# Feed-forward: several outputs share the early chunks, the late chunks follow; the last projection is stepped from an earlier place

## The chip, the cores and the metric

One core of a Trainium2 chip runs the whole program. The metric is the device time of one execution in microseconds (us). Six names recur: PE (the matmul engine; its weight loads are PEld), DVE (VectorE), ACT (ScalarE), POOL (GpSimd) and SP, whose queue (SPq) issues the DMAs spoken of here.

## The reference

The input x is 4096 rows of 256. An attention layer (16 heads of 16, causal) with its norms comes first and gives a new x; the feed-forward that the change touches follows:

```
x = x + layernorm(attention(layernorm(x)))
n = layernorm(x)
h = silu((n @ w1.T) * s1) * ((n @ w2.T) * s2)     # 256 -> 1024
h = gelu((h @ h1.T) * sh1)                        # 1024 -> 1024
h = gelu((h @ h2.T) * sh2)                        # 1024 -> 1024
y = (h @ w3.T) * s3                               # 1024 -> 256
x = x + layernorm(y)
```

The matrices w1, w2, h1, h2 and w3 hold -1, 0 and 1 alone.

## The kernel before

**Blocks and parts.** The 4096 rows are NB = 8 blocks of QB = 512. In the feed-forward, activations lie transposed: features on the 128 partitions, the block's 512 rows along the free axis. So 1024 features are FC = 8 chunks, 256 features are DC = 2. Since the matrices hold small whole numbers, each activation is split into a high part rounded to a matmul-friendly format and a low part that is the rest (`settle`, L974 to L978: a cast and a subtraction on DVE). Each product is thus made twice, once with each part, and both go into the same PSUM bank. The tiles are called ha (the output of w1/w2) and hb_0, hb_1 (those of h1 and h2), with h or l for the part. The function is built twice, for parts = 2 and parts = 1; a flag chooses at run time, and the profiled execution takes parts = 2.

**A block.** The loop over j goes through five stages, in this order on PE:

- w1/w2: for each of 8 outputs (oc), 4 matmuls into a bank za and 4 into a bank zb (`linear`, matmul at L1007). ACT applies silu to za (sl, L1046), DVE multiplies sl with zb (fa, L1048) and settles the result.
- h1: for each of 8 outputs, 16 matmuls (8 chunks, 2 parts) into a bank z. ACT applies gelu (fb, L1063) and DVE settles.
- h2: the same once more.
- the last projection of the feed-forward: for each of 4 row tiles t, 16 matmuls of 256 columns into a bank pyf (L1076). DVE multiplies by s3 (yf, L1083) and takes the norm's statistics (L138, L139).
- `leave`: the norm's root on POOL (rstd, L173), the normalisation on DVE (L1025), the addition of x on POOL (L1029) and the store to HBM on SP (L1032). In the last block it is done tile by tile.

Banks za, zb, z and pyf come in turn from a pool of six PSUM banks (`ps_f`); a bank is free again when ACT or DVE has read it. `f2` holds two tiles each of sl, and of the full result before it is split.

**The order.** A manual schedule is on for all five engines: the instructions of an engine run in the order in which the program's text issues them, and one that waits holds up everything behind it on its engine.

**Background work.** `Background` (L27) keeps a queue of generators. Each `step` runs the first of them to its next `yield`, and goes on to the next generator in the same step when the first has ended. `finish` runs all that is left. In the feed-forward there is a step after each output of w1/w2, h1 and h2, and two after those of h1 and h2 in block 1. Two kinds of work are in it:

- `project(NB - 1, room)` (L213), once, in block 1: the attention's last projection for the last block. Its pieces: a load of x and a load of the softmax sums (L222); after three empty steps the reciprocal on DVE (L225); then, in one piece, the store of the reciprocals (invd, L227) and four loads into oi (L231, L232), which share their buffers with the transposed input xTf of a block; after three empty steps two products on POOL (L239), a step each; two empty steps; two pieces of 8 matmuls py (L249), each with an addition and statistics on DVE (L258, L138); then the root (ve on DVE, L171, and rstd on POOL) and for each of four row tiles a normalisation and an addition on POOL (L177, L286); last, the store of the new x (L288).
- `norm_block(j + 1, ...)` (L291), in every block but the last: the load of the next block's x (L113), two empty steps, four pieces of statistics, then root and normalisation (yn, L177 on DVE) and in a last piece 8 transposing matmuls (ptf, L308) and the split into xTf (ACT L992, DVE L994).

In block 1 norm_block stands in the queue behind project.

Of the kernel before, what the change touches and what calls it, by code (L numbers as in the profile page):

```python
# [3 lines left out]

# [6 lines left out]
F32 = mybir.dt.float32  # L11
# [6 lines left out]
P = 128  # L18
QB = 512
NT = QB // P  # L20
# [47 lines left out]
def sandwich_kernel(  # L68
# [19 lines left out]
    nc = tc.nc  # L88
    S, D = x.shape
# [6 lines left out]
    NB = S // QB  # L96
    DC = D // P
    FC = F // P
# [37 lines left out]
    def layernorm_stats(src, mv, t):  # L136
        st = stat.tile([P, nc.vector.BN_STATS_DIM], F32, tag="bn", name="bn")
        nc.vector.bn_stats(st, src)  # L138
        nc.vector.bn_aggr(mv[:, t, :], st)  # L139
# [71 lines left out]
    PREP, PROJECT, NORM = 26, 28, 12  # L211
# [79 lines left out]
    def norm_block(j, room, done):  # L291

        xj = xb[j] = load_block(0, x1[j])
        for _ in range(3):
            yield True
        mv = stat.tile([P, NT, 2], F32, tag="mv", name=f"mvf_{j}")
        for t in range(NT):
            layernorm_stats(xj[:, t, :], mv, t)
            yield True
        rstd = layernorm_rstd(mv)  # L300
        xh = room.tokens(j)
        for t in range(NT):
            normalize(xh[:, t, :], xj[:, t, :], mv, rstd, t)
        yield True
        pts = [room.bank(f"ptf_{j}_{c}") for c in range(DC)]
        for c in range(DC):
            for t in range(NT):
                nc.tensor.transpose(  # L308
                    pts[c][:, t * P : (t + 1) * P], xh[:, t, c * P : (c + 1) * P], ident
                )  # L310
        done(pts)
        yield True
# [25 lines left out]
    with ExitStack() as actx:  # L338
# [13 lines left out]
        def two_banks(name):  # L352
            return ps_s.tile([P, 2, QB], F32, tag="s", name=name)
# [430 lines left out]
        bg = Background(lambda: unit_beside())  # L784
        halving = halve_weights()
        actx.enter_context(tc.manual_schedule(engines=ALL_ENGINES))
        room = Room()
# [26 lines left out]
        ahead, begun_pair, item = [], [], (0, 0)  # L814

        def unit_beside():
            j, g = item
            if not begun_pair and 1 <= j < NB - 1 and g < G - 1 and len(ahead) < NT:
                begun_pair.extend(next(stream))
                ahead.append(1)  # L820
            if begun_pair:
                issue(MaxUnit(*begun_pair.pop(0)))
# [6 lines left out]
        ps = two_banks("pb")[:, 0, 0:D]  # L829
        for c in range(DC):  # L830
            nc.tensor.matmul(
                ps,
                lhsT=bv[:, c : c + 1].to_broadcast([P, P]),
                rhs=wp[:, c, :],
                start=(c == 0),
                stop=(c == DC - 1),
# [73 lines left out]
    def feed_forward(halves):  # L910
# [5 lines left out]
        parts = 2 if halves else 1  # L916
        with ExitStack() as fctx:
# [4 lines left out]
            ps_f = fctx.enter_context(tc.tile_pool(name="ps_f", bufs=6, space=PSUM))  # L922
# [3 lines left out]
            def single(ap):  # L926

                return ap.bitcast(F32R) if halves else ap
# [15 lines left out]
            w3_r = fw.tile([P, FC, D], F32R, tag="w3", name=f"w3_{parts}")  # L944
            w3_sb = w3_r.bitcast(F32)
            room, bg = Room(), Background()
# [7 lines left out]
            def weights(key, oc, kc):  # L954

                if halves:
                    at = slice(oc % 4 * P, (oc % 4 + 1) * P)
                    return [tiles[key][c, oc // 4][:, at] for c in range(kc)]
                w = f2.tile([P, FC, P], F32, tag="raw", name=f"{key}_{oc}")
                src = sources[key][:, oc * P : (oc + 1) * P]  # L960
                nc.sync.dma_start(out=w[:, 0:kc, :], in_=src.rearrange("(c p) f -> p c f", p=P))
                return [w[:, c, :] for c in range(kc)]

            def activations(n, name):

                return [
                    (f1 if halves and n == DC else hp).tile(
                        [P, n, QB], F32, tag=f"h{n}{p}", name=f"{name}{p}"
                    )
                    for p in "hl"[:parts]  # L970
                ]

            def settle(dst, c, full):

                if halves:
                    hi, lo = (single(d[:, c, :]) for d in dst)
                    nc.vector.tensor_copy(hi, full)  # L977
                    nc.vector.tensor_tensor(lo, full, hi, ALU.subtract)  # L978

            def chunk(dst, c, name):  # L980

                if not halves:
                    return dst[0][:, c, :]
                return f2.tile([P, QB], F32, tag="full", name=name)
# [14 lines left out]
                            )  # L999
                return done  # L1000

            def linear(key, oc, src, kc, name):
                ps = ps_f.tile([P, QB], F32, tag="f", name=name)
                w = weights(key, oc, kc)
                for c in range(kc):
                    for i, part in enumerate(src):
                        nc.tensor.matmul(  # L1007
                            ps,
                            lhsT=w[c],
                            rhs=single(part[:, c, :]),  # L1010
                            start=(c == 0 and i == 0),
                            stop=(c == kc - 1 and i == parts - 1),
                        )
                return ps

            xTs[0] = [t.bitcast(F32) for t in xT0]
            if not halves:
# [21 lines left out]
            for j in range(NB):  # L1039
                xT = xTs[j]  # L1040
                ha = activations(FC, f"ha{parts}_{j}")
                for oc in range(FC):
                    za = linear("w1", oc, xT, DC, f"za{parts}_{j}_{oc}")
                    zb = linear("w2", oc, xT, DC, f"zb{parts}_{j}_{oc}")
                    sl = f2.tile([P, QB], F32, tag="sl", name=f"sl{parts}_{j}_{oc}")
                    nc.scalar.activation(sl, za, AF.Silu, scale=s1[:, oc : oc + 1])  # L1046
                    h = chunk(ha, oc, f"fa{parts}_{j}_{oc}")
                    nc.vector.scalar_tensor_tensor(  # L1048
                        h, zb, s2[:, oc : oc + 1], sl, ALU.mult, ALU.mult
                    )  # L1050
                    settle(ha, oc, h)
                    bg.step()
                if j == 1:
                    bg.add("project", project(NB - 1, room), PROJECT)
                if j + 1 < NB:
                    bg.add("norm", norm_block(j + 1, room, keep_features(j + 1)), NORM)
                src = ha
                for layer, (key, sc) in enumerate((("h1", sh1), ("h2", sh2))):
                    hb = activations(FC, f"hb{parts}_{j}_{layer}")
                    for oc in range(FC):  # L1060
                        z = linear(key, oc, src, FC, f"z{parts}_{j}_{layer}_{oc}")
                        h = chunk(hb, oc, f"fb{parts}_{j}_{layer}_{oc}")
                        nc.scalar.activation(h, z, AF.Gelu, scale=sc[:, oc : oc + 1])  # L1063
                        settle(hb, oc, h)
                        bg.step()
                        if j == 1:
                            bg.step()
                    src = hb
                bg.finish()
                y = f1.tile([P, NT, D], F32, tag="yf", name=f"yf{parts}_{j}")  # L1070
                mv = stat.tile([P, NT, 2], F32, tag="mv", name=f"mvo{parts}_{j}")
                for t in range(NT):
                    ps = ps_f.tile([P, QB], F32, tag="f", name=f"pyf{parts}_{j}_{t}")
                    for c in range(FC):
                        for i, part in enumerate(src):
                            nc.tensor.matmul(  # L1076
                                ps[:, 0:D],
                                lhsT=single(part[:, c, t * P : (t + 1) * P]),
                                rhs=(w3_r if halves else w3_sb)[:, c, :],
                                start=(c == 0 and i == 0),  # L1080
                                stop=(c == FC - 1 and i == parts - 1),
                            )
                    nc.vector.tensor_tensor(y[:, t, :], ps[:, 0:D], s3, ALU.mult)  # L1083
                    layernorm_stats(y[:, t, :], mv, t)
                    if j == NB - 1:

                        one = slice(t, t + 1)
                        due.append((j, y, mv, one, layernorm_rstd(mv[:, one, :])))
                        while len(due) > (t < NT - 1):
                            leave(*due.pop(0))  # L1090
                if j < NB - 1:
                    leave(j, y, mv, slice(0, NT), layernorm_rstd(mv))
# [3 lines left out]
    with tc.If(low < 1) as either:  # L1096
        feed_forward(True)
# [36 lines left out]
```

## Time and profile before

| what | us |
|---|---|
| median of 3 runs | 2488.5 |
| lowest and highest run | 2483.43, 2493.22 |
| profiled execution | 2495.86 |
| its span, first to last instruction | 2494.2 |
| first za matmul of the feed-forward | 1798.00 from the span's start |
| first pyf matmul of the last block | 2477.60 |

The page of the profile gives each engine's busy time and its share of the span. PE's row must be read with care: matmuls overlap, a 128x512 one is shown busy for 0.39 us while the next one starts 0.2266 us after it, so a gap in the starts can be larger than the idle time shown. Timelines list instructions in order of time, with the idle time of the engine before one and what ended it in brackets. Shares of time in the feed-forward by block, from the first matmul of each stage to that of the next, as the timeline gives them:

| block | w1/w2 | h1 | h2, with ptf | pyf to the next block |
|---|---|---|---|---|
| 0 | 15.04 | 29.05 | 30.81 | 8.15 |
| 1 | 14.53 | 34.86 (py in it) | 36.45 | 8.15 |
| 2 | 14.54 | 32.98 | 30.78 | 8.15 |
| 3 | 14.53 | 31.45 | 30.78 | 8.15 |
| 4 | 14.54 | 31.43 | 30.78 | 8.15 |
| 5 | 14.54 | 32.96 | 30.78 | 8.14 |
| 6 | 14.54 | 31.43 | 30.78 | 8.14 |
| 7 | 14.54 | 31.44 | 29.01 (no ptf) | - |

### The profile page before, as it was taken

The numbers are of one execution on the slowest core, as the hardware profiler recorded it, in microseconds if no ns is written. First come the engines' busy times: TensorE is split into PE (matmuls) and PEld (weight loads), VectorE is DVE, ScalarE is ACT, GpSimd is POOL, SyncE is SP. The second block draws the span as 40 slices with busy tenths as digits, with TensorE's granted clock in tenths as the row PEclk, the third lists the DMA queues.
The fourth block names the chain that finished last, engine by engine and source line by source line (L and its number), as shares of the span: only waits on it lengthen the run. The fifth ranks groups of instructions, "written<-read, shape, count | busy, mean of one in ns | idle before, by whom it ended". The sixth has DMA issues, their size and how long they took to land.

```text
span 2494.2 us, 40139 instructions
## 1 busy us (share of the span) xinstructions
PE 2395.7 (96%) x15237; PEld 1434.2 (58%) x15237; DVE 1786.7 (72%) x3838; ACT 1309.1 (52%) x1710; POOL 561.6 (23%) x898
## 2 busy tenths in 40 slices
PE   4899999999999999999999999999999999999998
PEld 2545545545554555455555555544488787887887
DVE  1667988888897989799999888986145535554553
ACT  1336666665675667666667667766822222222221
POOL 2325333423343233322422222000001200000000
PEclk8779999999999999999999999999999999999999
DMA  4444434323333322424222231111111100000000
GB/s 145 150 141 141 151 115 152 120 82 130 107 126 117 116 72 96 151 94 133 84 74 72 88 109 60 51 56 56 47 54 35 34 1 18 17 17 1 17 9 10
DMA packets 134825, 202.73 MB, mean 81 GB/s; under 512 B 14912, under 2 KB 59584, under 8 KB 134624
## 3 DMA queue, kind: packets, MB, share of 16 engines
q1 hardware_dynamic: 132672, 198.75, 24.3%
q8 instruction: 122, 2.00, 0.3%
q10 hardware_dynamic: 1776, 1.18, 0.2%
q14 instruction: 79, 0.65, 0.1%
q0 software_dynamic: 176, 0.15, 0.1%
HBM read 137.91 MB, written 62.13 MB: 80 GB/s over the span
## 4 chain that ended last, share of the span: by engine, by line
PE 82%; DVE 11%; issue 2%; DMA 2%; ACT 1%; POOL 1%; SPq 0%; ACTq 0%; POOLq 0%; DVEq 0%
PE av L714 20%; PE s L664 18%; PE z L1007 18%; PE pm L581 16%; DVE mx L594 3%; DVE pm L598 2%; PE pyf L1076 2%; DVE fa L1048 2%; PE pk L426 1%; PE py L249 1%; PE pv L543 1%; PE pq L426 1%; PE pmt L630 1%; PE za L1007 1%; PE zb L1007 1%
## 5 line engine op out<-in xcount | busy, mean ns | idle before, releaser
L679 ACT ACTIVATE e<-s 128x1024 f32<-128x1024 f32 (+3 forms) x1175 | 1039.1, 936 | 471.1 <-PE s L664 462.3
L594 DVE TENSOR_REDUCE mx<-pm 128x1 f32<-128x512 f32 x1792 | 1111.5, 682 | 153.0 <-PE pm L581 135.4
L581 PE MATMUL pm<-k,q 64*128 64x512 f32 (+3 forms) x2304 | 626.9, 456 | 33.0 <-DVE mx L594 18.6
L581 PEld LDWEIGHTS pm<-k,q 64*128 64x128 f32 x2304 | 325.1, 188 | 533.3 <-DVE mx L594 368.9
L714 PE MATMUL av<-e,v 128*32 128x512 f32 (+3 forms) x4608 | 582.5, 577 | 0.2 <-POOL e L684 0.2
L664 PE MATMUL s<-q,k 64*128 64x512 f32 (+3 forms) x2304 | 472.7, 391 | 4.4 <-ACT xT L533 1.2
L664 PE MATMUL s<-mrow,ones 64*128 64x512 f32 (+3 forms) x2304 | 458.9, 381 | 0.0
L598 DVE CUSTOM_DVE_ANT_0 pm<-pm,mask 128x384 f32<-128x384 f32 (+3 forms) x512 | 240.2, 517 | 78.6 <-PE pm L581 75.7
L1063 ACT ACTIVATE fb<-z,sh 128x512 f32<-128x512 f32 x128 | 88.1, 688 | 388.4 <-PE z L1007 367.2
L664 PEld LDWEIGHTS s<-q,k 64*128 64x128 f32 x2304 | 236.5, 189 | 71.7 <-issue 18.8
L664 PEld LDWEIGHTS s<-mrow,ones 64*128 64x128 f32 x2304 | 241.3, 189 | 38.3 <-DVE mrow L638 0.7
L684 POOL TENSOR_SCALAR_AFFINE_SELECT e<-e 128x256 f32<-128x256 f32 x256 | 102.3, 407 | 620.1 <-ACT e L679 618.0
L1007 PE MATMUL z<-hb_0h,h 128*128 128x512 f32 x512 | 200.8, 392 | 0.0
L1007 PE MATMUL z<-hb_0l,h 128*128 128x512 f32 x512 | 200.0, 391 | 0.0
L714 PEld LDWEIGHTS av<-e,v 128*32 128x32 f32 x4608 | 91.7, 108 | 143.6 <-issue 130.5
L173 POOL TENSOR_TENSOR rstd<-ve,neghalf 128x4 f32<-128x4 f32 (+1 forms) x22 | 20.7, 943 | 662.9 <-DVE ve L171 637.4
L977 DVE CAST hb_1h<-fb 128x512 fp32r<-128x512 f32 x64 | 27.8, 435 | 144.5 <-ACT fb L1063 144.5
L977 DVE CAST hb_0h<-fb 128x512 fp32r<-128x512 f32 x64 | 27.3, 427 | 138.7 <-ACT fb L1063 138.7
L1007 PEld LDWEIGHTS z<-hb_0h,h 128*128 128x128 f32 x512 | 96.8, 189 | 20.0
L1046 ACT ACTIVATE sl<-za,s 128x512 f32<-128x512 f32 x64 | 44.0, 689 | 122.2 <-PE za L1007 64.2
L1007 PEld LDWEIGHTS z<-hb_0l,h 128*128 128x128 f32 x512 | 96.7, 189 | 19.9
L1048 DVE SCALAR_TENSOR_TENSOR fa<-zb,s,sl 128x512 f32<-128x512 f32 x64 | 47.6, 745 | 72.2 <-ACT sl L1046 72.2
(247 smaller groups left out, 2437.8 us busy)
## 6 DMA issues: line engine op xcount, KB each, us to landing
k<-k SPq DMA_DIRECT2D x288, 256.0 KB
q<-q SPq DMA_DIRECT2D x64, 256.0 KB
x<-in_x_dram SPq DMA_DIRECT2D x16, 512.0 KB
k<-hik SPq DMA_DIRECT2D x32, 256.0 KB
k<-lok SPq DMA_DIRECT2D x32, 256.0 KB
q<-hiq SPq DMA_DIRECT2D x32, 256.0 KB
q<-loq SPq DMA_DIRECT2D x32, 256.0 KB
avd<-av_sb SPq DMA_DIRECT2D x32, 256.0 KB
```

The source lines that it names most:

```text
L426: nc.tensor.matmul(ps, lhsT=wqk[d][:, i * D + c * P : i * D + (c + 1) * P], rhs=xTs[j][:, d, :], start=(d == 0), stop=(d == DC - 1),)
L581: nc.tensor.matmul(ps[:, 0:n], lhsT=qT[j, g][pr][r, t * P : (t + 1) * P], rhs=kT[G * j + g, c, pr][r, 0:n], start=True, stop=True,)
L594: nc.vector.tensor_reduce(self.mx[:, h, c : c + 1], ps[:, 0:n], AX.X, ALU.max)
L598: nc.vector.tensor_tensor_reduce(out=ps[:, 0:n], in0=ps[:, 0:n], in1=mask[:, QB - n : QB], scale=1.0, scalar=-3.0e38, op0=ALU.add, op1=ALU ...
L664: nc.tensor.matmul(self.ps[i][:, self.q0 :], lhsT=(self.k, ones[pr])[m][r, :], rhs=(qT[j, g][pr], mT[j, g])[m][r, self.q0 :], start=(m == ...
L679: nc.scalar.activation(e[:, at : at + n, q0:], ps[:, :, q0:], AF.Exp)
L684: nc.gpsimd.affine_select(out=at, in_=at, compare_op=ALU.is_ge, fill=0.0, base=0, pattern=[[0, 2], [1, P]], channel_multiplier=-1,)
L714: nc.tensor.matmul(self.av[h * HW : (h + 1) * HW, q0:], lhsT=vb[kt // NT][:, kt % NT, o : o + HW], rhs=es[h // 2][:, h % 2, q0:], start=(k ...
L977: nc.vector.tensor_copy(hi, full)
L1007: nc.tensor.matmul(ps, lhsT=w[c], rhs=single(part[:, c, :]), start=(c == 0 and i == 0), stop=(c == kc - 1 and i == parts - 1),)
L1048: nc.vector.scalar_tensor_tensor(h, zb, s2[:, oc : oc + 1], sl, ALU.mult, ALU.mult)
L1063: nc.scalar.activation(h, z, AF.Gelu, scale=sc[:, oc : oc + 1])
```

## The change

`linear` becomes a generator over a list of outputs. It takes the banks of all of them at once, runs the first kc - late chunks for each output in turn, and then the last `late` chunks for each, handing an output over as it is complete. In h1, with two parts, the first three outputs are made so with late = 3: chunks 0 to 4 of outputs 0, 1 and 2, then chunks 5 to 7 of each. All other outputs of w1/w2, h1 and h2 are made as before. The last projection does the same with its first two row tiles and late = 2. The sums and their order within a bank stay as they were.

`project` is put into the queue of block 1 ahead of the loop over w1/w2, not behind it, so that loop's eight steps work on it; and behind each output of h1 and h2 in block 1 there are three steps, not two.

```diff
-            def linear(key, oc, src, kc, name):
-                ps = ps_f.tile([P, QB], F32, tag="f", name=name)
-                w = weights(key, oc, kc)
-                for c in range(kc):
-                    for i, part in enumerate(src):
-                        nc.tensor.matmul(ps, lhsT=w[c], rhs=single(part[:, c, :]),
...
-                return ps
+            def linear(key, ocs, src, kc, name, late=0):
+                banks = [ps_f.tile([P, QB], F32, tag="f", name=f"{name}_{oc}") for oc in ocs]
+                ws = [weights(key, oc, kc) for oc in ocs]
+                for cs in filter(len, (range(kc - late), range(kc - late, kc))):
+                    for ps, w in zip(banks, ws):
+                        for c in cs:
+                            for i, part in enumerate(src):
+                                nc.tensor.matmul(ps, lhsT=w[c], rhs=single(part[:, c, :]),
...
+                        if cs.stop == kc:
+                            yield ps
...
                 ha = activations(FC, f"ha{parts}_{j}")
+                if j == 1:
+                    bg.add("project", project(NB - 1, room), PROJECT)
                 for oc in range(FC):
...
                     bg.step()
-                if j == 1:
-                    bg.add("project", project(NB - 1, room), PROJECT)
                 if j + 1 < NB:
                     bg.add("norm", norm_block(j + 1, room, keep_features(j + 1)), NORM)
...
-                    for oc in range(FC):
-                        z = linear(key, oc, src, FC, f"z{parts}_{j}_{layer}_{oc}")
+                    ahead = 3 if halves and layer == 0 else 1
+                    name = f"z{parts}_{j}_{layer}"
+                    for oc, z in enumerate(
+                        chain(
+                            linear(key, range(ahead), src, FC, name, 3 if ahead > 1 else 0),
+                            *(linear(key, [oc], src, FC, name) for oc in range(ahead, FC)),
+                        )
+                    ):
...
-                        bg.step()
-                        if j == 1:
+                        for _ in range(1 + 2 * (j == 1)):
                             bg.step()
...
-                for t in range(NT):
-                    ps = ps_f.tile([P, QB], F32, tag="f", name=f"pyf{parts}_{j}_{t}")
-                    for c in range(FC):
...
+                def outputs(ts, late=0):
+                    banks = {t: ps_f.tile([P, QB], F32, tag="f", name=f"pyf{parts}_{j}_{t}") for t in ts}
+                    for cs in filter(len, (range(FC - late), range(FC - late, FC))):
+                        for t, ps in banks.items():
+                            for c in cs:
...
+                            if cs.stop == FC:
+                                yield t, ps
+                for t, ps in chain(outputs(range(2), 2), *(outputs([t]) for t in range(2, NT))):
                     nc.vector.tensor_tensor(y[:, t, :], ps[:, 0:D], s3, ALU.mult)
```

More of the change, by code (lines that the diff above doesn't have):

```diff
@@ L2 @@
 from contextlib import ExitStack
-from itertools import cycle
+from itertools import chain, cycle
 import concourse.bass as bass
@@ L1000, in keep_features @@
                 return done
-            def linear(key, oc, src, kc, name):
-                ps = ps_f.tile([P, QB], F32, tag="f", name=name)
-                w = weights(key, oc, kc)
-                for c in range(kc):
-                    for i, part in enumerate(src):
[L1007 to L1013, printed above, removed]
-                return ps
+            def linear(key, ocs, src, kc, name, late=0):
[5 more added lines that the diff above has]
+                            for i, part in enumerate(src):
+                                nc.tensor.matmul(
+                                    ps,
+                                    lhsT=w[c],
+                                    rhs=single(part[:, c, :]),
+                                    start=(c == 0 and i == 0),
+                                    stop=(c == kc - 1 and i == parts - 1),
+                                )
+                        if cs.stop == kc:
+                            yield ps
             xTs[0] = [t.bitcast(F32) for t in xT0]
@@ L1041, in feed_forward @@
                 ha = activations(FC, f"ha{parts}_{j}")
+                if j == 1:
+                    bg.add("project", project(NB - 1, room), PROJECT)
                 for oc in range(FC):
-                    za = linear("w1", oc, xT, DC, f"za{parts}_{j}_{oc}")
-                    zb = linear("w2", oc, xT, DC, f"zb{parts}_{j}_{oc}")
+                    za, = linear("w1", [oc], xT, DC, f"za{parts}_{j}")
+                    zb, = linear("w2", [oc], xT, DC, f"zb{parts}_{j}")
                     sl = f2.tile([P, QB], F32, tag="sl", name=f"sl{parts}_{j}_{oc}")
@@ L1059, in feed_forward @@
                     hb = activations(FC, f"hb{parts}_{j}_{layer}")
-                    for oc in range(FC):
-                        z = linear(key, oc, src, FC, f"z{parts}_{j}_{layer}_{oc}")
+                    ahead = 3 if halves and layer == 0 else 1
[4 more added lines that the diff above has]
+                            *(linear(key, [oc], src, FC, name) for oc in range(ahead, FC)),
+                        )
+                    ):
                         h = chunk(hb, oc, f"fb{parts}_{j}_{layer}_{oc}")
@@ L1071, in feed_forward @@
                 mv = stat.tile([P, NT, 2], F32, tag="mv", name=f"mvo{parts}_{j}")
-                for t in range(NT):
-                    ps = ps_f.tile([P, QB], F32, tag="f", name=f"pyf{parts}_{j}_{t}")
-                    for c in range(FC):
[L1075 to L1082, printed above, removed]
+                def outputs(ts, late=0):
[3 more added lines that the diff above has]
+                            for c in cs:
+                                for i, part in enumerate(src):
+                                    nc.tensor.matmul(
+                                        ps[:, 0:D],
+                                        lhsT=single(part[:, c, t * P : (t + 1) * P]),
+                                        rhs=(w3_r if halves else w3_sb)[:, c, :],
+                                        start=(c == 0 and i == 0),
+                                        stop=(c == FC - 1 and i == parts - 1),
+                                    )
+                            if cs.stop == FC:
+                                yield t, ps
+                for t, ps in chain(outputs(range(2), 2), *(outputs([t]) for t in range(2, NT))):
                     nc.vector.tensor_tensor(y[:, t, :], ps[:, 0:D], s3, ALU.mult)
```

## The prediction

> **What bounds the kernel now.** First the page: which engine is full.
>
> ```profile
> PE 2395.7 (96%) x15237; PEld 1434.2 (58%) x15237; DVE 1786.7 (72%) x3838; ACT 1309.1 (52%) x1710; POOL 561.6 (23%) x898
> ```
>
> PE carries the chain that ended last (82% of it). The programs of both kernels are the same up to the feed-forward, so only 1798.00 (first za) to 2494.2 can change. There I asked who PE waited for; the columns are total us, times, longest.
>
> ```profile
> PE ptf L308 <- DVE yn L177: 3.7, 1, 3.7
> PE pyf L1076 <- DVE hb_1l L978: 1.8, 8, 0.2
> PE z L1007 <- DVE ha_7h L977: 0.9, 2, 0.6
> ```
>
> These idles look like pennies, but matmuls overlap: a 128x512 one is busy 0.39 and the next starts 0.2266 later. So I read start to start. PE's timeline where block 1 begins h1:
>
> ```profile
> 1898.08 0.39 PE L1007 MATMUL z<-ha_1l,h 128*128 128x512 f32 x1
> 1898.65 0.50 PE L1007 MATMUL z<-ha_1h,h 128*128 128x512 f32 x1 [0.18 <-DVE ha_1h L977]
> 1899.37 0.51 PE L1007 MATMUL z<-ha_1l,h 128*128 128x512 f32 x1 [0.22 <-DVE ha_1l L978]
> 1900.50 0.50 PE L1007 MATMUL z<-ha_1h,h 128*128 128x512 f32 x1 [0.62 <-DVE ha_1h L977]
> 1901.22 0.50 PE L1007 MATMUL z<-ha_1l,h 128*128 128x512 f32 x1 [0.22 <-DVE ha_1l L978]
> 1901.56 0.39 PE L1007 MATMUL z<-ha_1h,h 128*128 128x512 f32 x1
> ```
>
> Output 0 needs chunks 6 and 7 while DVE still makes them. Its 16 matmuls start at 1895.58, the next output's at 1901.56: 5.98 instead of 3.63, so 2.35 lost. Then the granted clock, from the table of windows (us; PE, PEld, DVE, ACT, POOL; PEclk; DMA):
>
> ```profile
> 1895.58:1901.56 5.98, 4.73 (x18) 2.92 (x16) 5.38 (x10) 1.98 (x2) 0.00 (x0) 1.00 0.00 0
> 1952.20:1961.10 8.90, 5.16 (x17) 3.99 (x16) 3.96 (x9) 1.86 (x3) 1.03 (x1) 0.62 0.00 0
> 1989.58:1998.60 9.02, 7.77 (x24) 5.32 (x23) 6.49 (x12) 2.66 (x3) 0.00 (x0) 0.82 0.01 2
> 2062.00:2076.00 14.00, 14.00 (x63) 11.60 (x62) 12.37 (x23) 4.82 (x7) 4.04 (x5) 1.00 0.23 75
> ```
>
> Block 2's stall (third row) is followed by a slow stretch, matmuls 0.43 apart for some 3.4 us; block 1's (first row) is not.
>
> **Late chunks in h1 (removes a stall).** From first z<-ha to first z<-hb, the timeline gives block 0 29.05 us (128 x 0.2266: no stall) and blocks 2 to 7 32.98, 31.45, 31.43, 32.96, 31.43, 31.44. Above 29.03 that is 3.95, 2.42, 2.40, 3.93, 2.40, 2.41: 17.5 together, of which some 3.0 are the slow stretches in blocks 2 and 5. The same 128 matmuls run after; three outputs first take chunks 0 to 4 (30 x 0.2266 = 6.80 us), then the rest. Chunk 5 is wanted 6.80 after the start, chunk 7 7.7 after; in block 1 chunk 7's low half came 5.6 after (1901.2 - 1895.58), in block 3 5.7. About 2 us of cover: stall zero. Next in line is a bank: output 1 starts 2.27 after and takes zb 5's, freed 0.7 after (fa 5 ends 1896.28). DVE meets three outputs 1.36 apart with 1.1 us of work each and keeps up. **-17.5**; block 1 -2.35.
>
> **Late chunks in the last projection.** The start-to-start of pyf matmuls is 0.12, but output 0 loses (1875.08 - 1874.58) - 0.12 = 0.38 and then 0.11: 0.49 per block. After, chunk 6 is wanted 24 x 0.12 = 2.9 us after the start, and chunk 7's low half is ready 2.1 after (1875.0). In the last block the gain does not reach the end: outputs 0 and 1 come 0.48 apart, DVE spends 1.3 on each plus 0.40 on the leaving one, and output 3 reaches DVE at 2485.95 as before. 7 x 0.49 = **-3.4**.
>
> The skill speaks against such interleaving: Trainium skill, "TensorE: Matmul & The Clock Gate", "A second HAM failure mode: psum-queue depth-cycling", tells of a kernel that cycled through banks and whose clock kept dropping. The row decides: w1/w2 changes bank every 4 matmuls and the window 2062 to 2076 has clock 1.00. By the row it costs 0; by the rule, if all 48 interleaved h1 matmuls of a block ran 0.2 later each, 8 x 48 x 0.2 = +77. I take the row.
>
> **The projection, block 1 alone.** Its work does not grow; steps come earlier and denser. Pieces, counted from the generator: 4 reciprocal, 5 the DMAs, 9 and 10 POOL's products, 13 and 14 the 16 py matmuls (3.26 us), 15 to 18 rstd and POOL's eight operations, 19 the store; then norm: 1 load, 4 to 7 statistics, 8 yn, 9 ptf. Before: two pieces per z, py behind the 7th output of h1, ptf behind the 6th of h2. After (the built program's order agrees): reciprocal behind w1/w2's 4th, DMAs behind its 5th, py behind h1's 2nd output, ve behind its 3rd, ptf behind its 7th.
>
> *Reciprocal* (outputs counted from 0 here): SP still issues the load of the sums behind block 0's store (1888.22), 5.5 us before DVE needs it at 1893.68, and block 2's x took 4.4. It puts 0.55 of DVE ahead of fa 4. fa 4 frees zb 4's bank, which zb 7 takes (six banks); it ended at 1894.42, zb 7 began at 1894.68. Slack 0.2: **+0.35**, h1 starts at 1895.93.
>
> *DMAs.* All are SP's, in order:
>
> ```profile
> 1907.75 0.34 SPq L227 DMA_DIRECT2D invd<-sums  x1
> 1908.20 0.67 SPq L231 DMA_DIRECT2D oi_2h<-avd  x1
> ...
> 1911.64 0.57 SPq L232 DMA_DIRECT2D oi_2l<-invd  x1
> ...
> 1919.43 1.29 POOL L239 TENSOR_TENSOR oi_2h<-oi_2h,oi_2l 128x512 f32<-128x512 f32 x1 [3.73 <-DMA oi_2l<-invd]
> ```
>
> oi shares its buffers with xTf, which block 1's w1/w2 read: the first oi load waits for zb 7, about 1895.95. From that issue to POOL's second product took 11.2, from the last issue 7.8; so 1905.95 to 1907.2, say 1906.5, done 1907.85. PE reaches py after 42 matmuls, 1895.93 + 9.51 = 1905.44, does the first chunk's 0.4 and waits: **+2.0** (1.5 to 2.7). Py ends at 1910.7, h1's 3rd output at 1912.05.
>
> *From ve to ptf.* The timeline of the same stretch before:
>
> ```profile
> 1932.48 0.16 DVE L171 TENSOR_SCALAR ve<-mvy 128x4 f32<-128x4 f32 x1
> ...
> 1941.97 0.74 POOL L286 TENSOR_TENSOR yn<-yn,x 128x256 f32<-128x256 f32 x1
> ...
> 1943.14 0.51 SPq L113 DMA_DIRECT2D x<-x  x1
> ...
> 1947.58 0.43 DVE L138 BATCH_NORM_STATS2 bn<-x 128x6 f32<-128x256 f32 x1 [0.50 <-DMA x<-x]
> ```
>
> POOL takes 10.2, SP can issue the load of block 2's x only behind the store that waits for POOL, and the load lands 4.4 later: 15.1 from ve to the first statistics. Behind these on DVE, in order: settle 6th (1.07), three statistics (1.74), settle 7th (1.07), ve, POOL's rstd, yn; ve to ptf was 1.87. Sum 15.1 + 0.58 + 3.88 + 1.87 = 21.4. After: DVE ends py's sums 2.45 behind py, as before (1929.03 - 1926.58), at 1913.15, settles h1's 3rd output (1.1) and does ve at 1914.3; ptf at 1935.7. PE has four outputs to cover it: 1912.05 + 4 x 3.625 = 1926.55. Wait **9.2**, where before it was 3.9 (1956.11 - 1951.98 - 0.23): **+5.3**. The waiting statistics hold settles 6 and 7 on DVE; nothing but ptf needs them earlier. A slow stretch follows as it did before: 0.
>
> Block 1: -2.35 - 0.2 (first matmuls after py) + 0.35 + 2.0 + 5.3 = **+5.1**.
>
> **Sum** -17.5 - 3.4 + 5.1 = **-15.8**. The span goes from 2494.2 to 2478.4; 1.7 lie outside it, so the profiled execution from 2495.9 to 2480.1; from the median shown, 2488.5: **2472.7**.
>
> The clock, a second rule: the same page, "HAM oscillation", puts the limit at PE gaps over about 3.4 us. Rows differ: blocks 2 and 5 slowed after gaps of at most 1.13 between starts, four others with the same gaps did not. By the rule py's 2 us wait costs nothing more, by the rows 1.5 in one of three cases; I take 0 and keep 1.5 for the range.
>
> **Rivals.**
> A, the forecast: starts filled, block 1 pays 3 to 8 (waits 1 us off in either direction, slow stretch or not): -18 to -13; 2470 to 2476. **0.57.**
> B, pacing works: POOL and the load finish in time and both waits go. Block 1 then gains 2.35 + 5.7 (its h2, 36.45 against the others' 30.77) - 0.35 = 7.7: -28.6, **2460**. For it: the projection starts 14.5 us sooner. Against: 21.4 of chain over 14.5 of PE. **0.10.**
> C, block 1 pays 9 to 13: oi's loads land 3 us later beside the store and the x load, POOL slows where DVE works (yn took 1.66 beside a DVE cast, else 1.22), and both waits end in a slow clock: -10, **2478.5**, no change within what can be told. **0.24.**
> D, the starts are not filled since what DVE lacks is throughput (72% of the span): the wait moves to fa's banks. Against: blocks 1 to 7 lose the same 2.4, and DVE idles between h1's outputs. Block 1's loss alone: +5 - 3, **2490**. **0.05.**
> E, slower: interleaved banks halve the clock; at 0.2 per matmul it eats the 15.8 from 79 slow matmuls on (10 of 48 per block), and if all are slow +77 - 16: **2550**. Against: w1/w2's clock of 1.00. **0.04.**
>
> Half a per cent, 12.4 us, is about what a measurement tells from no change: faster means under 2476.1. A lies almost wholly below, with B, and C at the edge. Faster 0.70, same 0.25, slower 0.05. The range takes in A, most of C and part of B: **2463 to 2481**.
>
> **What would show it.** h1 of blocks 2 to 7 at 29.0 with clock 1.00; pyf without its 0.5 step; zb 7 late by 0.3; py waiting for POOL's oi some 2; ptf waiting for yn some 9, and "PE ptf <- DVE yn" at the head of PE's waits. Wrong it would be if h1 still stalls (which bank?), if the ptf wait is under 4 (then B), or if py waits over 4.

## The result, and the profile after

| | before | after |
|---|---|---|
| median of 6 runs, us | 2488.73 | 2473.47 |
| lowest and highest run | 2483.43, 2493.61 | 2469.77, 2475.10 |
| span of the profiled execution | 2494.2 | 2471.0 |
| of it, from the first za on | 696.2 | 677.15 |

The ratio on record, over the fast runs, is 0.9927, with a 95% interval of 0.9916 to 0.9938. The two medians shown, 15.3 us apart, stand at 0.9939, just outside it; so the size of the gain is known to a few us and no better. The profiled executions differ by 23.2 us, but 4.15 of these lie ahead of the feed-forward, where the two programs are the same (first za at 1798.00 before, at 1793.85 after). What the change did is the other 19.05. The timeline by stage, from the first matmul of one stage to that of the next, shows where (the table of before is in the section on its profile):

| block, after | w1/w2 | h1 | h2, with ptf | pyf to the next block |
|---|---|---|---|---|
| 0 | 15.04 | 29.05 | 30.81 | 7.67 |
| 1 | 14.54 | 44.93 (py, ptf in it) | 29.01 (no ptf) | 7.68 |
| 2 | 14.53 | 29.01 | 30.82 | 7.67 |
| 3 | 14.53 | 29.02 | 30.81 | 7.67 |
| 4 | 14.54 | 29.01 | 30.78 | 7.67 |
| 5 | 14.54 | 29.01 | 30.78 | 7.67 |
| 6 | 14.54 | 29.01 | 30.81 | 7.68 |
| 7 | 14.53 | 29.01 | 29.02 | - |

h1 of blocks 2 to 7 went from 191.69 to 174.07 together: -17.62. The last projection of blocks 0 to 6 went from 57.03 to 53.71: -3.32. From the last block's first pyf to the end it was 16.6 and is 15.8: -0.8. Of that, 0.48 is steady: DVE's last instruction ends 11.67 after the first pyf before, 11.18 after it now, and so (11.66 to 11.67, 11.18 to 11.19) in all 13 traces of this study. The rest lies behind it, in the last store and the program's end, which took between 4.6 and 5.2 in these traces with old and new starts alike; that part is chance. Block 1's h1 and h2 went the other way, from 71.31 to 73.94: +2.63. That makes -19.1, against -19.05 for the whole.

The page's row for PE has the same share as before, 96%. In the feed-forward its busy time fell too, from 672.70 to 660.17, although the matmuls are the same, because part of a stall counts as busy (in the first stall that the forecast shows, 2.35 us were lost and 1.25 were idle). So the row's share says little of what was gained:

```profile
PE 2376.2 (96%) x15237; PEld 1430.6 (58%) x15237; DVE 1784.5 (72%) x3838; ACT 1309.0 (53%) x1710; POOL 561.9 (23%) x898
```

Who PE waited for in the feed-forward (us in total, times, longest):

```profile
PE ptf L308 <- DVE yn L177: 8.5, 1, 8.5
PE za L1010 <- ACT av_sb L723: 0.7, 1, 0.7
```

The lines of z and of pyf have gone from this view; ptf's has grown from 3.7 to 8.5. PE's own timeline where the new order meets the late chunks in block 1 (the stage began at 1890.96, chunk 5 of output 0 is wanted 6.8 us later):

```profile
1897.53 0.39 PE L1010 MATMUL z<-ha_1l,h 128*128 128x512 f32 x1
1897.76 0.39 PE L1010 MATMUL z<-ha_1h,h 128*128 128x512 f32 x1
1897.98 0.39 PE L1010 MATMUL z<-ha_1l,h 128*128 128x512 f32 x1
1898.21 0.39 PE L1010 MATMUL z<-ha_1h,h 128*128 128x512 f32 x1
1898.44 0.39 PE L1010 MATMUL z<-ha_1l,h 128*128 128x512 f32 x1
1898.66 0.39 PE L1010 MATMUL z<-ha_1h,h 128*128 128x512 f32 x1
```

Every start is 0.226 after the one before it. The table of windows (us; PE, PEld, DVE, ACT, POOL busy; granted clock; DMA) for block 1's first 42 matmuls of h1, for the wait of ptf with what follows it, and for the whole h1 of block 3:

```profile
1890.96:1900.48 9.52, 9.52 (x44) 7.88 (x42) 6.18 (x11) 2.67 (x3) 2.70 (x2) 1.00 0.32 110
1919.62:1934.30 14.68, 6.21 (x20) 4.68 (x19) 6.96 (x19) 1.86 (x3) 1.03 (x1) 0.65 0.14 43
2069.14:2098.16 29.02, 29.02 (x130) 24.03 (x128) 15.36 (x32) 6.79 (x9) 0.00 (x0) 1.00 0.00 1
```

The clock is 1.00 throughout the interleaved banks; of these three windows only the one behind the wait of ptf has a lower one. In block 1 the projection's loads, the load of block 2's x, the statistics that wait for it and ptf, each from the timeline of its engine:

```profile
1890.96 0.67 SPq L231 DMA_DIRECT2D oi_2h<-avd  x1
...
1899.47 1.28 POOL L239 TENSOR_TENSOR oi_2h<-oi_2h,oi_2l 128x512 f32<-128x512 f32 x1 [1.41 <-DMA oi_2l<-invd]
...
1907.37 0.16 DVE L171 TENSOR_SCALAR ve<-mvy 128x4 f32<-128x4 f32 x1
...
1916.85 0.73 POOL L286 TENSOR_TENSOR yn<-yn,x 128x256 f32<-128x256 f32 x1
...
1918.02 0.51 SPq L113 DMA_DIRECT2D x<-x  x1
...
1922.36 0.43 DVE L138 BATCH_NORM_STATS2 bn<-x 128x6 f32<-128x256 f32 x1 [7.40 <-DMA x<-x]
...
1928.47 2.21 PE L308 MATMUL ptf<-ident,yn 128*128 128x128 f32 x8 [8.46 <-DVE yn L177]
```

The statistics' bracket now holds 7.40, where it was 0.50 before: DVE stands in front of the load with the settling of later outputs behind it. From ve to ptf it is 21.1 us.

### The profile page after: what moved, and what is told of

Its sections match the earlier page's. It is cut to its first block, busy times and chain, and to the rows that moved or that the text cites. A ratio compares the mean times of both kernels' runs of the same rounds, so it can differ in the third digit from the quotient of the medians.

```text
span 2471.0 us, 40139 instructions
## 1 busy us (share of the span) xinstructions
PE 2376.2 (96%) x15237; PEld 1430.6 (58%) x15237; DVE 1784.5 (72%) x3838; ACT 1309.0 (53%) x1710; POOL 561.9 (23%) x898
## 4 chain that ended last, share of the span: by engine, by line
PE 86%; DVE 8%; issue 2%; DMA 2%; POOL 1%; ACT 1%; SPq 0%; ACTq 0%; POOLq 0%; DVEq 0%
PE av L714 20%; PE s L664 18%; PE z L1010 18%; PE pm L581 16%; DVE mx L594 3%; DVE pm L598 2%; PE za L1010 2%; PE zb L1010 2%; PE pyf L1089 2%; PE py L249 1%; PE pk L426 1%; PE pv L543 1%; PE pq L426 1%; PE pmt L630 1%; PE ptf L308 1%
## 5 line engine op out<-in xcount | busy, mean ns | idle before, releaser
L581 PE MATMUL pm<-k,q 64*128 64x512 f32 (+3 forms) x2304 | 624.2, 453 | 32.7 <-DVE mx L594 19.1
```

Of the source, the lines that this page charges most:

```text
L581: nc.tensor.matmul(ps[:, 0:n], lhsT=qT[j, g][pr][r, t * P : (t + 1) * P], rhs=kT[G * j + g, c, pr][r, 0:n], start=True, stop=True,)
```

## The experiments

Each was timed against the kernel before on its own chip. A column "feed-forward" gives the profiled execution from its first za to its end, which the noise ahead of it does not touch. It has chance of its own: the slow stretches, some 1.5 each, a wait in block 0 (below), and what lies behind DVE's last instruction.

| kernel | feed-forward | h1 of blocks 2 to 7, each | block 1, h1 and h2 | ptf waits (block 1) | ratio to before, 95% interval |
|---|---|---|---|---|---|
| before | 696.2 | 31.4 to 33.0 | 71.31 | 3.74 | |
| before, again | 697.46 | 31.4 to 33.1 | 70.93 | 3.74 | |
| the change | 677.15 | 29.0 | 73.94 | 8.46 | 0.9927 (0.9916 to 0.9938) |
| starts only | 671.78 | 29.0 | 68.56 | 3.74 | 0.9908 (0.9881 to 0.9936) |
| pacing only | 702.91 | 31.4 to 33.1 | 78.19 | 8.56 | 1.0015 (1.0005 to 1.0025) |
| outgoing block on POOL | 680.55 | 29.4 | 69.46 | 3.74 | 0.9927 (0.991 to 0.9943) |
| two ahead | 679.73 | 29.1 to 29.2 | 75.13 | 8.48 | one run |
| two steps | 671.63 | 29.0 | 67.96 | 3.75 | one run |
| load early | 677.08 | 29.0 | 73.88 | 8.24 | one run |
| load into a free tile | 674.30 | 29.0 | 70.59 | 3.74 | one run |
| paced apart | 667.16 | 29.0 | 63.98 | 0.80 | 0.988 (0.9859 to 0.99) |
| paced apart, second chip run | 667.54 | 29.0 | 63.98 | 0.80 | 0.9888 (0.9866 to 0.991) |
| starts, apart | 667.43 | 29.0 | 63.99 | 0.80 | 0.9882 (0.9861 to 0.9902) |

The theory was that of the forecast: the filled starts earn all of it, and the moved projection costs. The rival was that pacing (the earlier place and the third step) earns, or at least is free.

**The kernel before, again.** No edit.

> The kernel before, unchanged, for a second trace. Theory (slow stretches fall by chance): all of blocks 1 to 7 stall 2.4 us at the start of h1 again, but the blocks whose h1 takes 33 instead of 31.4 us are others than 2 and 5, or another number of them. Rival (they belong to the place): blocks 2 and 5 again. If the time differs by several us from 2495.9, most of it should lie before the feed-forward or in these stretches.

Slow stretches came in blocks 2 and 6 (h1 32.92 and 33.06) instead of 2 and 5. So they fall by chance, about 1.5 us each, and a single trace of before carries 3 us of luck in its sum.

Block 0, which had not stalled in the first trace, lost 1.9 here (30.94). DVE's first cast of block 0 shows why; the lines are of before, before again and the change:

```profile
1802.16 0.43 DVE L977 CAST ha_0h<-fa 128x512 fp32r<-128x512 f32 x1
1802.52 0.43 DVE L977 CAST ha_0h<-fa 128x512 fp32r<-128x512 f32 x1 [2.04 <-DMA h<-r_h]
1800.01 0.43 DVE L977 CAST ha_0h<-fa 128x512 fp32r<-128x512 f32 x1 [2.12 <-DMA h<-r_h]
```

In 8 of the 13 traces this cast waited 1.1 to 2.1 us for a DMA (which one is not settled: it waits for several), and DVE was late by that much. Where the starts are the old ones, h1 of block 0 then lost 1.1 to 1.9 (three traces of three: before again, pacing only, outgoing block on POOL); where they are filled it took 29.04 to 29.05 all the same (five of five, the change among them). So the filled starts also cover a late block 0, which neither the forecast nor the profiled pair counts, since before's one trace had no such wait.

The first za came at 1796.44; over the 13 traces of this study, with the same instructions ahead of it, it came between 1786.97 and 1799.62.

**The two parts alone.** Starts only: the projection goes back.

```diff
-                if j == 1:
-                    bg.add("project", project(NB - 1, room), PROJECT)
                 for oc in range(FC):
...
+                if j == 1:
+                    bg.add("project", project(NB - 1, room), PROJECT)
                 if j + 1 < NB:
...
-                        for _ in range(1 + 2 * (j == 1)):
+                        for _ in range(1 + (j == 1)):
```

> Late chunks in h1 and in the last projection alone; the projection of the last block stays where it was, with two steps per output. Theory (the starts earn all, the moved projection costs 5): feed-forward some 24 us shorter than before and 5 shorter than with the whole change; ptf in block 1 waits 3.9 us as before. In all 0.990 to 0.991 of before. Rival (moving the projection is what earns): no better than 0.995, slower than the whole change.

Pacing only: the other half.

```diff
-                    ahead = 3 if halves and layer == 0 else 1
+                    ahead = 1
...
-                for t, ps in chain(outputs(range(2), 2), *(outputs([t]) for t in range(2, NT))):
+                for t, ps in chain(*(outputs([t]) for t in range(NT))):
```

> The moved projection with three steps alone; all outputs made whole, one after the other. Theory: h1 of blocks 1 to 7 stalls 2.4 us as before (with or without a slow stretch of 1.5), ptf in block 1 waits 8.6 us, so 5 us longer than before: 1.001 to 1.003. Rival (pacing helps): under 0.999.

Both came out as the theory had it. The parts add up: -0.92% and +0.15% give -0.77%, the whole gave -0.73%. The starts alone have a feed-forward 5.4 us shorter than the change; the moved projection alone makes it 5.5 longer than before, again (block 1 alone 7.3, of which some 1.5 is a slow stretch at the start of its h1). The wait is seen in the waits of PE, first row starts only, second pacing only:

```profile
PE ptf L308 <- DVE yn L177: 3.7, 1, 3.7
```

```profile
PE ptf L308 <- DVE yn L177: 8.6, 1, 8.6
```

**Why the starts stalled: the outgoing block on POOL.** The kernel before, with one engine changed in `leave`; nothing interleaved.

```diff
-                    nc.vector.tensor_scalar(
+                    (nc.vector if j == NB - 1 else nc.gpsimd).tensor_scalar(
                         y[:, t, :], y[:, t, :], mv[:, t, 0:1], rstd[:, i : i + 1],
```

> The kernel before, with the normalisation of the outgoing block (yf, blocks 0 to 6) on POOL instead of DVE; nothing else. Theory (DVE enters w1/w2 behind by the outgoing block's work, and h1's start pays for it): h1 of blocks 1 to 7 takes 29.0 to 29.3 us without any late chunks; 0.992 to 0.994. Rival (DVE needs 1.86 us per output where PE needs 1.81, so it is behind in any case): h1 still stalls 1 us or more.

h1 takes 29.36 to 29.40 in blocks 2 to 7: the stall of 2.4 is down to 0.35, just above the span that was expected and far below the rival's. So DVE is late for h1 mainly since the previous block's normalisation, and the wait for its root, stand at the head of w1/w2 in its queue. In block 1, whose w1/w2 begins at 1881.05 before and at 1880.59 here, DVE does this before:

```profile
1883.68 2.23 DVE L1025 TENSOR_SCALAR yf<-yf,mvo,rstd 128x256 f32<-128x256 f32 x4 [1.12 <-POOL rstd L173]
1885.83 0.74 DVE L1048 SCALAR_TENSOR_TENSOR fa<-zb,s,sl 128x512 f32<-128x512 f32 x1
```

and this with the outgoing block on POOL:

```profile
1882.69 0.75 DVE L1048 SCALAR_TENSOR_TENSOR fa<-zb,s,sl 128x512 f32<-128x512 f32 x1 [0.60 <-PE zb L1007]
```

The first fa comes 2.10 after the stage's start instead of 4.78. The measured gain, 0.9927, equals that of the whole change, by another road; the two together were not tried. Block 0 lost 1.7 here (30.79) for the other reason, the DMA: its first cast waited 1.90.

**How deep the interleaving must be: two ahead.**

```diff
-                    ahead = 3 if halves and layer == 0 else 1
+                    ahead = 2 if halves and layer == 0 else 1
```

> The whole change with two outputs sharing the early chunks in h1 instead of three. Theory (chunk 7's low half comes 5.6 us after the start and is wanted 5.66 after): h1 of blocks 2 to 7 takes 29.0 to 29.2. Rival (the third output's cover is needed): over 29.5.

29.12 to 29.23: two outputs cover all but 0.1 to 0.2. The third is the margin.

**What ptf waits for: two steps.** The forecast summed one chain from ve to ptf, 21.4 us. The edit is one line:

```diff
-                        for _ in range(1 + 2 * (j == 1)):
+                        for _ in range(1 + (j == 1)):
```

> The whole change with two steps per output in block 1 instead of three; root and transposes stand behind the same output (the 2nd of h2). Theory (same output: ptf must wait for gelu, settling, root, yn): ptf waits 3.7 to 3.9 us, as in the kernel before. Rival (the sum of the forecast, 21.4 us of chain from ve over six outputs of cover): ptf waits 1.9 us or less.

The waits of PE in this kernel:

```profile
PE ptf L308 <- DVE yn L177: 3.8, 1, 3.8
```

The feed-forward, 671.63, is that of starts only, 671.78: the earlier place costs nothing, and what costs the change its 5.4 us is the third step. The rival fell, and with it the forecast's picture of one chain. With ve behind h1's 4th output and ptf behind h2's 2nd, six outputs lie between; a chain of 21.4 would have left 1.9. The wait is 3.75, that of before. There, too, the root's piece and the piece with the transposes stood behind the same output, so PE, done with that output, waits until gelu, settling, ve, POOL's rstd and the first yn have followed it (before: last z started 1951.98, gelu 1952.45, ve 1954.24, yn 1955.55, ptf 1956.11). However early the rest is, this remains.

**The load, twice.** First the load of block 2's x was put ahead of the store, with the matmuls of py:

```diff
         y = room.tokens(j)
+        if last:
+            early.add(2)
+            xb[2] = load_block(0, x1[2])
...
-        xj = xb[j] = load_block(0, x1[j])
+        xj = xb[j] = xb[j] if j in early else load_block(0, x1[j])
```

> The whole change, but the load of block 2's x is issued with the matmuls of py, ahead of the store that waits for POOL; three steps as in the change. Theory (two waits in a row: 4.7 for the load, 3.9 for root and transposes behind the same output): ptf waits 3.9 us instead of 8.5. Rival (the load is all of it): ptf waits under 1 us. Rival (POOL's own work is): still over 7.

This did not test what it was to test. SP's timeline of this kernel:

```profile
1923.55 0.36 SPq L113 DMA_DIRECT2D x<-x  x1
1923.96 0.50 SPq L293 DMA_DIRECT2D x<-yn  x1
```

The load is ahead of the store, but only 0.4 us ahead: it was given the buffer of the last block's x, which POOL's last addition releases (1922.79 + 0.74 = 1923.53). So the store was not all that held the load; the buffer held it as well. The second try loads into block 0's transposed input, which is free by then:

```diff
+            xb[2] = xT0[0].bitcast(F32).rearrange("p c (a d) -> p (c a) d", d=D)
+            nc.sync.dma_start(out=xb[2], in_=rows(x1[2], 0))
```

> The load of block 2's x is issued with the matmuls of py again, this time into a tile that is free by then (block 0's transposed input), so that it waits neither for POOL's additions, nor for the buffer of the last block's x, nor for the store; three steps as in the change. Theory (two waits in a row: 4.7 for the load, 3.7 for root and transposes behind the same output): the statistics no longer wait, ptf waits 3.7 to 3.9 us. Rival (the load is all): under 1 us. Rival (POOL's own work is): still over 7.

The rest of the edit is that of the first try. DVE's timeline around the first statistics, then the waits of PE:

```profile
1918.49 0.69 DVE L984 TENSOR_TENSOR hb_0l<-fb,hb_0h 128x512 fp32r<-128x512 f32 x1
1919.10 0.42 DVE L138 BATCH_NORM_STATS2 bn<-xT0h 128x6 f32<-128x256 f32 x1
```

```profile
PE ptf L314 <- DVE yn L177: 3.7, 1, 3.7
PE py L255 <- POOL oi_2h L241: 1.9, 1, 1.9
```

No bracket stands behind the statistics: they wait for nothing. ptf waits 3.7, so the 8.5 of the change are 4.7 for the load and 3.7 for the two pieces behind one output. A new wait came up that nobody had expected in this run: py for oi, 1.9 us. The early load stands in the queue right behind the four loads of oi, and the last of these took longer beside it (first issue to POOL's second product 10.5, against 8.5 in the change). That the additional load is what slowed them was not tried separately.

**Apart.** The moved projection with two steps, and one empty piece more, so that the root stands behind one output and the transposes behind the next:

```diff
-                        for _ in range(1 + 2 * (j == 1)):
+                        for _ in range(1 + (j == 1)):
...
         xj = xb[j] = load_block(0, x1[j])
-        for _ in range(3):
+        for _ in range(4 if j == 2 else 3):
```

> The whole change, but two steps per output in block 1 and one more empty piece in norm_block there, so that statistics end behind one output and the transposes come behind the next one. Theory (ptf waits since the root and the transposes stand behind the same output, and since the load lands late; both are cured here): ptf waits under 0.5 us, no slow stretch, h1 and h2 of block 1 take 63 to 64 us instead of 73.9; 10 us better than the whole change, 0.988 to 0.990 of before. Rival (the load's lateness sets the wait however the pieces lie): ptf still waits 2 us or more.

```profile
PE ptf L308 <- DVE yn L177: 0.8, 1, 0.8
```

0.80, not under 0.5, since DVE still has the last row tile's statistics (0.42 and 0.18) to do between that output's settling and ve; but no slow stretch, and block 1's h1 and h2 take 63.98. It is 10.0 us better than the change in the feed-forward. Then the same empty piece with the projection at its old place (both edits are shown above, starts only and the empty piece), beside a second run of the kernel with the moved one:

> Late chunks in h1 and in the last projection, the last block's projection at its old place with two steps per output, and one more empty piece in norm_block of block 1, so that the root and the transposes stand behind different outputs. Theory (that piece is what block 1 needed; moving the projection earns nothing): ptf waits 0.3 to 0.8 us, feed-forward within 1 us of the kernel with the moved projection and the same empty piece, both 0.987 to 0.990 of before. Rival (the early place is worth something): 3 us or more behind it.

> The moved projection with two steps and one more empty piece, once more, for comparison on one chip with the kernel in which the projection stays at its old place. Feed-forward 667 us as before, 0.986 to 0.990 of before.

667.43 and 667.54: with the empty piece it makes no difference where the projection begins. The early place earned nothing. With the projection at its old place, the empty piece alone takes the feed-forward from 671.78 (starts only) to 667.43. Both versions beat the change and the kernel before, at 0.988 to 0.989 of before.

## Why the prediction was right, and where not

The forecast said 2472.7 and 2473.47 was measured, which is nearer than its terms deserve: in the profiled pair the feed-forward moved by 19.05, not 15.8, and the medians' nearness to the forecast is in part luck. Term by term, against the profiled executions:

| term | forecast | measured |
|---|---|---|
| h1 of blocks 2 to 7 | -17.5 | -17.6 |
| last projection, blocks 0 to 6 | -3.4 | -3.3 |
| tail of the last block | 0 | -0.8 (0.48 of it steady) |
| block 1: stall of h1 | -2.35 | -2.35 (gone) |
| block 1: reciprocal | +0.35 | 0 |
| block 1: py waits for oi | +2.0 | 0 |
| block 1: first matmuls after py | -0.2 | 0 |
| block 1: ptf waits | +5.3 | +4.7 |
| block 1: slow stretch behind ptf | 0 | +0.3 |
| block 1 in all (h1 and h2) | +5.1 | +2.63 |
| sum | -15.8 | -19.05 |

**The starts were right** in mechanism and size, by the reading of starts instead of idle time: the waits of before summed to some 9 us for z in all its rows, the starts said 17.5 with the clock. Three of these belong to the slow stretches of that one trace. With the single stretch of another trace (pacing only, block 5) it would have been 16; with none 14.5. Block 0 draws the other way: its "no stall" was read from the one trace with old starts, of four, in which the first cast did not wait, and covering it is worth 1.1 to 1.9 in the others. So one pair of traces tells the gain to some 3 us only. The interval, 15.4 to 20.9 us, holds the pair's 19.05; the forecast's 15.8 lies at its lower end.

**The weighing of the two rules** that the forecast cites. By the rule on cycling through banks the forecast put the change at +77; the row (w1/w2, clock 1.00) said 0. In all nine traces with interleaved h1 the stage took 29.0 to 29.2 in each of blocks 2 to 7, and the windows above show clock 1.00. The row was right, and rival E is out. The other rule, by which gaps under about 3.4 us leave the clock alone, is contradicted by the stalls of before: in three traces with the old starts (before, before again, pacing only) 6 of the 21 starts of h1 in blocks 1 to 7 were followed by a slow stretch, behind idle times of at most 0.63 each. py's wait of 2 us did not come in the change. It came in the kernel that loads into a free tile, 1.93, and there the clock held, as the forecast had taken it (the window from py to the first z):

```profile
1902.52:1907.98 5.46, 3.53 (x17) 2.79 (x16) 4.02 (x7) 0.69 (x1) 1.49 (x1) 1.00 0.14 43
```

That is one case.

**Reciprocal: wrong.** The step took the six banks as a strict ring, so that zb 7 would wait for fa 4. In the trace of after zb 7 starts at 1890.05, while fa 4 runs from 1889.52 to 1890.17. So its bank was not the one that fa 4 frees. In the trace zb 7 waits for ACT alone, whose last read before it, of za 5, ended at 1888.74. w1/w2 took 14.54 as before, and where the 0.55 on DVE made chunks late, the filled start covered it. In pacing only, whose starts are not filled, the first late gap of block 1's h1 is 0.94 between starts against 0.57 before: there the term's size seems to show, but the reciprocal was not tried apart.

**py for oi: a size.** The issue of the first oi load behind zb 7 was as foreseen. But from there to POOL's second product it took 8.5 instead of 11.2, which the forecast had read from before, and which contained 1.5 of SP waiting for the store of the reciprocals between the loads. Where the other 1.2 went was not followed up. POOL's second product ended at 1900.75, just as PE came to the second chunk (py began at 1900.48), so the wait of 2.0 vanished with nothing to spare. The -0.2 behind py did not come: the first two z there start 0.42 apart, before and after.

**ptf: size nearly right, picture wrong.** 8.62 lost between the starts (8.85 - 0.23) where 9.2 was forecast; from ve to ptf it was 21.1 where 21.4 was forecast. But the forecast took the wait as what is left of one chain when PE's outputs have covered the rest. The runs show a part of 3.7, before and after, that no cover removes, because two pieces stand behind one output. That is why it did not ask for the cheap remedy, and why its rival B ("both waits go") was argued from cover alone. The slow stretch behind ptf was a little longer than before: from ptf to the tenth z behind it 5.81, against 5.53. The load's part, 4.7, hangs on POOL through the store and through a buffer; the forecast named the first alone.

**The tail: wrong by 0.48.** It was taken that DVE, with two row tiles at once, would reach the last one at the same time as before. It needed 1.2 for the first tile and 1.5 for the next two with the leaving one in them, not 1.3 and 1.7, and took the last one 7.87 after the stage's start (2463.11 - 2455.24) instead of 8.35.

Rivals B and C did not happen: block 1 neither gained nor paid 9. D is out since the stall is gone; its idea that DVE lacks throughput is answered by the kernel with the outgoing block on POOL.

## What to carry to other kernels

Read start to start, not idle time, where an engine overlaps its own instructions; the stall of 2.4 us per block showed as 1.2 to 1.3 of idle. When work is cut into pieces that are slipped in between others, it is less the pace than the seam that counts: two pieces that depend on each other through three other engines must not come behind the same output. Here one empty piece between them earned 4.4 us of the feed-forward, while the denser pacing cost 5.4. Before an earlier start is given to background work, ask what its last step waits for, the buffer as well as the queue.

## What was not expected of the hardware

The part ahead of the feed-forward, with the same instructions in the same order, varied by 12.7 us between 13 executions, more than twice what the third step cost; parts of a program that do not change are the first thing to take out of a comparison of two traces. The clock's slow stretches came behind stalls made of idle times of 0.2 to 0.6 us, in 6 of 21 like cases, and never (0 of 54) where h1 was interleaved and lost 0.2 at most.
